# Moving the last stage's norm scaling to GpSimd and its masked factors to ScalarE

## Chip, cores and metric

The kernel runs on one core of a Trainium2 chip. The metric is device time in microseconds for one launch, the median of several runs. The engines are TensorE (PE in the profile; PEld is its weight load), VectorE (DVE), ScalarE (ACT), GpSimd (POOL) and SyncE (SP, which here only issues transfers). Each engine works through its own queue in order; engines meet through semaphores.

## What is computed

Four graph layers over x of shape (128, 128, 128): 128 batches of 128 nodes with 128 features, with a 0/1 adjacency of the same shape. Each layer is `x = x + layer(relu(layernorm(x)))`. The change touches only the part of the kernel that computes the end of layer 1 and all of layers 2 and 3. Cut to what matters:

```
# end of layer 1: y is normalised over all batches, leaky relu, second half of the product with Wt, added to x
# layer 2 (four heads) and layer 3 (one head, followed by elu):
h  = max(layernorm(x), 0)
Wh = h @ W (+ b)
e  = leaky_0.2(Wh.a_i[:, None] + Wh.a_j[None, :])
e  = where(adj > 0, e, very negative)
x  = x + softmax(e) @ Wh            # layer 3: x + elu(softmax(e) @ Wh)
```

## The kernel before

The batches are worked in 32 groups of four (`G = 4`), each held as a tile of 128 nodes by four batches by 128 features. Two long stages come first: layer 0 with the pairwise differences of layer 1, until about 1500 us, and the scores and softmax of layer 1, until about 2317 us. The last stage begins there and ends with the kernel; it finishes layer 1 and does layers 2 and 3 for one group after another, with several groups in flight. Its code is `attention(g)`.

`attention(g)` does no work itself. It lists steps: a name, an engine, a cost in microseconds, the steps that must come before, the PSUM banks that it takes and gives back, and the work. `_planned` merges the lists of all groups into a single order: it repeatedly takes the step that could start first by these costs, with an allowance of 0.2 us from engine to engine, a release of one more group every `PERIOD = 12` us (five at the beginning), four single PSUM banks (`ONE = 4`) and two double ones (`TWO = 2`). The work is issued in that order, so the costs decide how each engine's queue is sorted; what the chip then takes is another matter. SBUF tiles rotate through rings (`BUFS`: seven for h, ten for off, five for right2, two for right3).

The steps of a group, with the lines of the profile:

- lz and lx load y and x (SP); for five groups they are on the chip already. off (line 1190, GpSimd) turns the stored uint8 mask M8 into a bf16 tile that is 1 where there is no edge and 0 where there is one. M8 holds only 0 and 1, written as `adj > 0`.
- y (line 1193, ScalarE), yl (line 1195, VectorE), po (line 1201, TensorE) and x1 (line 1204, VectorE) finish layer 1.
- Then `layer(n, ...)` runs for layer 2 and, after the attention of layer 2 and its addition x2, for layer 3. mv (lines 1217 and 1219, VectorE) takes mean and variance. rs (lines 225, 226, 1223 and 1224, GpSimd) makes the inverse root rs and the shift nb = -mean x rs. h (line 1229, ScalarE) is relu(x rs + nb), four instructions of 128x128, as scale and shift differ by batch. pt (line 1235, TensorE) transposes h into PSUM; hT (line 1304, ScalarE) copies it back; pr (lines 1241 and 1244) multiplies by the weights.
- v (line 1252, VectorE) takes the score columns, w1 (lines 1257, 1258 and 1261, GpSimd) prepares the ones beside the values and wr (lines 1267 and 1270, ScalarE) copies the values. sp (lines 1283 and 1285, GpSimd) splits the scores into three bf16 pieces, and pe (line 1290, TensorE) transposes them.
- left (line 1312, ScalarE) copies the first half of pe. right (line 1296, VectorE) spreads the second half over four parts, each multiplied by its column of a 0/1 tile `own`, so that each part keeps only the rows of its own head or batch.
- ps (lines 1332 and 1335 in layer 2, 1372 and 1375 in layer 3, TensorE) adds the scores, left times right, and the mask: off times a diagonal of a very negative number.
- e (lines 1318 and 1319, ScalarE: two exponentials), em (line 1322, VectorE: the larger of the two), w and pv (lines 1345 and 1381, TensorE), o (lines 1359, 1360, 1385 and 1386, VectorE), x2 (line 1365) and in layer 3 ex (line 1395, ScalarE), x3 and x4 (lines 1396 and 1398, VectorE). out stores x (SP).

Line 960, in the stage before, makes another tile from the same mask with a product and a sum on GpSimd.

Of the kernel before, what the change touches and what calls it, by code (L numbers as in the profile page):

```python
# [11 lines left out]
BF16 = mybir.dt.bfloat16  # L12
U8 = mybir.dt.uint8
AF = mybir.ActivationFunctionType
OP = mybir.AluOpType
AX = mybir.AxisListType

P = 128
G = 4
# [149 lines left out]
def tile_gnn_stack(ctx: ExitStack, tc: tile.TileContext, a: dict, out: bass.AP):  # L169
    nc = tc.nc  # L170
# [46 lines left out]
    M8 = [res.tile([P, G, P], U8, tag=f"m{g}", name=f"m{g}") for g in range(NG)]  # L217
# [44 lines left out]
    with tc.tile_pool(name="c0", bufs=1) as c0, tc.tile_pool(name="p0", bufs=2) as p0, ExitStack() as ctx0:  # L262
# [383 lines left out]
        with tc.If(nc.values_load(flag, min_val=0, max_val=1) > 0) as cmp, \  # L646
# [6 lines left out]
            for g in range(NG):  # L653
                x = pr.tile([P, G, P], F32, name="x")
# [5 lines left out]
                hT = pr.tile([P, G, P], F32, name="hT")  # L660
# [111 lines left out]
    with tc.tile_pool(name="bn", bufs=1) as bn:  # L772
# [3 lines left out]
        last = bn.tile([P, 1], F32, name="last")  # L776
# [41 lines left out]
    with tc.tile_pool(name="c1", bufs=1, reuse_waits="tile") as c1, \  # L818
# [8 lines left out]
        own = c1.tile([P, 1], F32, name="own")  # L827
# [19 lines left out]
        for n in range(2):  # L847
            t = c1.tile([P, G, 1 + 2 * KH], F32, name=f"sk{n}")
# [296 lines left out]
    with tc.If(nc.values_load(bounded, min_val=0, max_val=1) > 0) as cmp, \  # L1145
# [10 lines left out]
        def attention(g):  # L1156


            t, steps = {}, []

            def step(name, engine, cost, after, work, takes=(), last=()):
                steps.append(((g, name), engine, cost, [(g, n) for n in after], takes, last, work))

            def sb(name, shape, dtype=F32):
                t[name] = p3.tile(shape, dtype, tag=name, bufs=BUFS[name], name=name)
                return t[name]
# [20 lines left out]
            lx = () if on_chip else ("lx",)  # L1187

            def masked():
                nc.gpsimd.tensor_scalar(sb("off", [P, G, P], BF16), M8[g], 0.0, None, op0=OP.is_equal)  # L1190

            step("off", "Pool", 1.5, lx, masked)
            step("y", "ACT", 0.75, () if on_chip else ("lz",), lambda: nc.scalar.activation(
                t["y"], t["y"], AF.Identity, bias=bias2, scale=scale2[:, 0:1]))
            step("yl", "DVE", 0.65, ("y",), lambda: nc.vector.scalar_tensor_tensor(
# [2 lines left out]
            def rest():  # L1198
                po = bank("po")
                for k in range(G):  # L1200
# [4 lines left out]
                 last=("po",))  # L1205

            def layer(n, heads, wx, first):

                q = lambda name: name + str(n)
                N = P + 2 * heads  # L1210
                mv, rs, nb = q("mv"), q("rs"), q("nb")
# [14 lines left out]
                def normed():  # L1226
                    h = sb("h", [P, G, P])
                    for k in range(G):
                        nc.scalar.activation(h[:, k, :], t["x"][:, k, :], AF.Relu, bias=t[nb][:, k:k + 1],  # L1229
                                             scale=t[rs][:, k:k + 1])  # L1230

                def turned():
                    pt = bank(q("pt"))
# [59 lines left out]
                rows, own = (32 * G, own_h) if first else (32, own_k)  # L1293

                def right():
                    nc.vector.tensor_tensor(sb(q("right"), [P, 4, P], BF16)[0:rows],
                                            t[q("pe")][0:rows, 1:2, :].to_broadcast([rows, 4, P]),
                                            own[0:rows, :, None].to_broadcast([rows, 4, P]), OP.mult)

                step(mv, "DVE", 1.05, ("x1",) if first else ("x2",), moments)  # L1300
                step(rs, "Pool", 1.7, (mv,), root)
                step(q("h"), "ACT", 1.2, (rs,), normed)
                step(q("pt"), "PE", 0.5, (q("h"),), turned, takes=(q("pt"),))
                step(q("hT"), "ACT", 0.52, (q("pt"),), lambda: nc.scalar.copy(sb(q("hT"), [P, G, P]), t[q("pt")]),
                     last=(q("pt"),))
                step(q("pr"), "PE", 1.0, (q("hT"),), projected, takes=("2" + q("pr"),))
                step(q("v"), "DVE", 0.3, (q("pr"),), scores)
# [3 lines left out]
                step(q("pe"), "PE", 0.2, (q("sp"),), crossed, takes=(q("pe"),))  # L1311
                step(q("left"), "ACT", 0.3, (q("pe"),), lambda: nc.scalar.copy(
                    sb(q("left"), [P, P], BF16)[0:rows], t[q("pe")][0:rows, 0, :]))
                step(q("right"), "DVE", 0.6, (q("left"),), right, last=(q("pe"),))

            def exps(ps, e):

# [3 lines left out]
            def higher(ps, e):  # L1321
                nc.vector.scalar_tensor_tensor(t[e], t[e], TINY, t[ps], op0=OP.max, op1=OP.max)  # L1322

            layer(2, 4, w2x, True)
            for k in range(G):
                ps, e, pv = f"ps{k}", f"e{k}", f"pv{k // 2}"
# [39 lines left out]
                t["x"], t["o2"], -1.0, t["x"], op0=OP.add, op1=OP.add))  # L1366

            layer(3, 1, w3x, False)

            def summed3():  # L1370
# [33 lines left out]
        with tc.manual_schedule():  # L1404
            groups = [attention(g) for g in sorted(range(NG), key=lambda g: g not in Y)]
            for work in _planned(groups, PERIOD, {"1": ONE, "2": TWO}):
                work()


    with cmp.Else(), tc.tile_pool(name="c2", bufs=1) as c2, tc.tile_pool(name="p2", bufs=5) as p2, \  # L1410
# [25 lines left out]
        left = c2.tile([3, 4], F32, name="left")  # L1436
# [188 lines left out]
```

## Time and profile before

| what | value |
|---|---|
| median of 3 runs | 2777.38 us (2776.46 to 2777.83) |
| profiled execution | 2781.11 us, of which span 2779.3 us |
| granted TensorE clock, mean | 0.968 |
| PE busy over the span | 2457.4 us (88%) |
| DVE busy | 2472.0 us (89%) |
| ACT busy | 2388.7 us (86%) |
| POOL busy | 1724.0 us (62%) |
| last stage, 2317 to 2777 us: busy PE, DVE, ACT, POOL | 402.2, 381.1, 382.6, 252.7 of 460 us |

The profiled execution is one run, 3.7 us above the median of the others. Busy shares are averages over three stages with different limits, so only the last row speaks of the stage around the change. Where instructions of an engine follow each other closely, their durations overlap, and the distance from start to start says what one of them costs the engine.

### The profile page before, as it was taken

To read this page: it belongs to the slowest core of one execution; us is meant where nothing else is said; L and a number is where in the kernel's file an instruction comes from. 1 tells how busy PE (TensorE), PEld (TensorE's weight loads), DVE (VectorE), ACT (ScalarE), POOL (GpSimd) and SP (SyncE) were. 2 spreads that over 40 slices of the span, in tenths; PEclk is the share of its full clock that TensorE was granted. 3 is DMA by queue.
4 is the path that set the end of the run, shared out by engine and by line. 5 is a ranking of instruction groups with operands and counts; after the bars stand their busy time and mean duration, and the time that the engine had idled before them with its cause. 6 is when DMAs were issued, how large, how long until landed. Compare 5 with 4: busy or idle time off the path is not lost.

```text
span 2779.3 us, 42065 instructions
## 1 busy us (share of the span) xinstructions
PE 2457.4 (88%) x14521; PEld 1182.0 (43%) x14521; DVE 2472.0 (89%) x4712; ACT 2388.7 (86%) x2837; POOL 1724.0 (62%) x1629
## 2 busy tenths in 40 slices
PE   3899999999999999999998789888888897999896
PEld 2333333333333333333332344444444445777675
DVE  4899999999999999999999688888888887899976
ACT  4899999999999999999998778778778766899985
POOL 5799999999999999999997001111000115565642
PEclk7999999999999999999999899999999999999998
DMA  7455555555555555555543899999999971121110
GB/s 283 171 223 201 212 201 210 210 212 201 208 201 208 211 209 207 208 207 215 206 193 125 330 409 411 410 411 410 409 410 410 409 266 54 46 69 58 58 31 25
DMA packets 195933, 635.66 MB, mean 229 GB/s; under 512 B 32755, under 2 KB 100470, under 8 KB 132214
## 3 DMA queue, kind: packets, MB, share of 16 engines
q1 hardware_dynamic: 195264, 632.62, 58.6%
q8 instruction: 120, 1.97, 0.3%
q14 instruction: 111, 0.91, 0.1%
q10 hardware_dynamic: 438, 0.17, 0.0%
HBM read 328.84 MB, written 303.89 MB: 228 GB/s over the span
## 4 chain that ended last, share of the span: by engine, by line
ACT 33%; PE 22%; DVE 19%; issue 11%; DMA 10%; POOL 3%; SPq 1%; ACTq 0%; DVEq 0%; POOLq 0%
ACT d L360 11%; ACT z L336 11%; PE hp L322 6%; PE ps L871 5%; DMA rows<-sk 4%; DVE d L312 3%; DMA u<-rows 3%; DVE z L914 3%; DMA z<-hp 3%; PE hp L325 2%; ACT h L1229 2%; PE pk L878 2%; PE pv L1345 2%; ACT o L462 1%; ACT h L503 1%
## 5 line engine op out<-in xcount | busy, mean ns | idle before, releaser
L312 POOL TENSOR_TENSOR d<-xe 128x2048 f32<-128x2048 f32 x256 | 1074.1, 4202 | 67.1 <-PE hp L322 48.9
L322 PE MATMUL hp<-d,w1T 128*64 128x512 f32 x4096 | 999.4, 603 | 119.8 <-ACT z L336 96.8
L360 ACT ACTIVATE d<-d 128x2048 f32<-128x2048 f32 x384 | 734.6, 1935 | 24.7 <-POOL d L312 18.2
L312 DVE TENSOR_TENSOR d<-xe,xp 128x2048 f32<-128x2048 f32 x256 | 579.5, 2264 | 5.8 <-PE hp L322 3.1
L322 PEld LDWEIGHTS hp<-d,w1T 128*64 128x64 f32 x4096 | 286.2, 137 | 640.4 <-issue 466.6
L336 ACT COPY z<-hp 128x1024 f32<-128x1024 f32 x512 | 516.9, 1028 | 47.1 <-PE hp L325 24.4
L962 POOL TENSOR_TENSOR x<-x,bt 128x512 f32<-128x512 f32 x32 | 46.5, 1455 | 672.1 <-DMA x<-x 629.0
L350 DVE BATCH_NORM_STATS2 st<-z 128x6 f32<-128x512 f32 x512 | 349.3, 682 | 42.4 <-ACT z L336 42.1
L351 DVE BATCH_NORM_STATS2 st<-z 128x6 f32<-128x512 f32 (+1 forms) x512 | 329.3, 643 | 0.0
L914 DVE SCALAR_TENSOR_TENSOR z<-z 128x2048 f32<-128x2048 f32 x128 | 296.6, 2317 | 6.5 <-ACT z L896 6.5
L896 ACT ACTIVATE z<-z,bias,scale 128x2048 f32<-128x2048 f32 x128 | 267.1, 2087 | 9.3 <-DVE bias L809 7.7
L325 PE MATMUL hp<-both_t,xw 128*64 128x512 f32 x1024 | 268.3, 596 | 0.0
L900 ACT ACTIVATE zr<-z,bias,scale 128x2048 f32<-128x2048 f32 x128 | 267.3, 2088 | 0.9 <-DMA z<-hp 0.9
L871 PE MATMUL ps<-z,w2z 128*32 128x512 f32 x1024 | 144.7, 638 | 65.1 <-DVE z L914 64.9
L878 PEld LDWEIGHTS pk<-pick,su 128*128 128x128 f32 x1024 | 127.4, 196 | 136.2 <-DVE su L892 94.0
L878 PE MATMUL pk<-pick,su 128*128 128x16 f32 x1024 | 139.9, 269 | 19.9 <-DVE su L892 19.3
L1345 PE MATMUL pv<-wr,e 128*128 128x128 f32 x1024 | 141.7, 285 | 5.8 <-DVE e L1322 4.0
L871 PE MATMUL ps<-z,w2l 128*32 128x512 f32 x1024 | 142.7, 626 | 0.0
L871 PE MATMUL ps<-zr,w2r 128*32 128x512 f32 x1024 | 141.0, 623 | 0.0
L325 PEld LDWEIGHTS hp<-both_t,xw 128*64 128x64 f32 x1024 | 80.7, 138 | 140.7 <-issue 140.7
L1345 PEld LDWEIGHTS pv<-wr,e 128*128 128x128 f32 x1024 | 129.4, 197 | 13.5 <-DVE e L1322 4.1
L1322 DVE SCALAR_TENSOR_TENSOR e<-e,ps 128x512 f32<-128x512 f32 x160 | 106.8, 677 | 25.9 <-ACT ps L1319 25.1
(243 smaller groups left out, 3823.2 us busy)
## 6 DMA issues: line engine op xcount, KB each, us to landing
hp<-z SPq DMA_DIRECT2D x248, 1024.0 KB, 3.9
z<-hp SPq DMA_DIRECT2D x248, 1024.0 KB, 14.2
x<-x SPq DMA_DIRECT2D x118, 256.0 KB, 5.9
u<-rows SPq DMA_DIRECT2D x32, 384.0 KB, 11.6
x<-in_x_dram SPq DMA_DIRECT2D x32, 256.0 KB, 3.1
adj<-in_adj_dram SPq DMA_DIRECT2D x32, 256.0 KB, 3.5
part<-in_adj_dram SPq DMA_DIRECT2D x16, 512.0 KB, 7.6
out_dram<-x SPq DMA_DIRECT2D x32, 256.0 KB, 2.4
```

The lines of the kernel that those rows point to most:

```text
L312: eng.tensor_tensor(d, ahead, x[:, None, None, :].to_broadcast([P, 2, KC, P]), OP.max if t == BY_MAX else OP.subtract)
L322: nc.tensor.matmul(hp[64 * hh:64 * hh + 64, c:c + 512], w1T2 if by_max else w1T, d[:, hh, c:c + 512], start=True, stop=not by_max, skip_gr ...
L325: nc.tensor.matmul(hp[64 * hh:64 * hh + 64, c:c + 512], XW[i // NT // 2][:, i // NT % 2, :], both_t.rearrange("p h k i -> p h (k i)")[:, h ...
L336: nc.scalar.copy(half_of(b, t), linear.pop(i))
L350: nc.vector.bn_stats(st[:, 2 * t, :], hs[:, 0:512])
L351: nc.vector.bn_stats(st[:, 2 * t + 1, :], hs[:, 512:1024 - P * last])
L360: nc.scalar.activation(diffs[i], diffs[i], AF.Abs)
L871: nc.tensor.matmul(ps[32 * c:32 * c + 32, :], w[:, w0:w0 + 32], v[:, 512 * c:512 * c + 512], start=j0 == 0, stop=w is w2r, skip_group_chec ...
L878: nc.tensor.matmul(pk[:, kk, 0:16], su[:, kk, :], pick.rearrange("p h j -> p (h j)"), start=True, stop=True)
L900: nc.scalar.activation(zr, z1, AF.Relu, bias=bias1, scale=scale1[:, 0:1])
L914: nc.vector.scalar_tensor_tensor(z0, z0, 0.01, z0, op0=OP.mult, op1=OP.max)
L1345: nc.tensor.matmul(t[pv][:, k % 2, hd, :], t[e][:, hd, :], flat[:, at:at + P], start=True, stop=True)
```

## The change

Four edits, all in `attention(g)`:

- off is computed as mask x (-1) + 1 instead of mask == 0, still on GpSimd, and its planned cost goes from 1.5 to 0.65.
- h of both layers becomes x rs + nb without relu, four tensor_scalar instructions on GpSimd instead of four activations on ScalarE; planned cost 1.9 instead of 1.2.
- The relu moves into hT, the copy of the transposed h out of PSUM, which stays on ScalarE at the same planned cost.
- right becomes four activations on ScalarE, each with a column of `own` as its scale, instead of one product on VectorE; planned cost 1.4 instead of 0.6.

```diff
             def masked():
-                nc.gpsimd.tensor_scalar(sb("off", [P, G, P], BF16), M8[g], 0.0, None, op0=OP.is_equal)
-
-            step("off", "Pool", 1.5, lx, masked)
+                nc.gpsimd.tensor_scalar(sb("off", [P, G, P], BF16), M8[g], -1.0, 1.0, op0=OP.mult, op1=OP.add)
+
+            step("off", "Pool", 0.65, lx, masked)
...
                 def normed():
                     h = sb("h", [P, G, P])
                     for k in range(G):
-                        nc.scalar.activation(h[:, k, :], t["x"][:, k, :], AF.Relu, bias=t[nb][:, k:k + 1],
-                                             scale=t[rs][:, k:k + 1])
+                        nc.gpsimd.tensor_scalar(h[:, k, :], t["x"][:, k, :], t[rs][:, k:k + 1], t[nb][:, k:k + 1],
+                                                op0=OP.mult, op1=OP.add)
...
                 def right():
-                    nc.vector.tensor_tensor(sb(q("right"), [P, 4, P], BF16)[0:rows],
-                                            t[q("pe")][0:rows, 1:2, :].to_broadcast([rows, 4, P]),
-                                            own[0:rows, :, None].to_broadcast([rows, 4, P]), OP.mult)
+                    to = sb(q("right"), [P, 4, P], BF16)
+                    for part in range(4):
+                        nc.scalar.activation(to[0:rows, part, :], t[q("pe")][0:rows, 1, :], AF.Identity,
+                                             scale=own[0:rows, part:part + 1])
...
-                step(q("h"), "ACT", 1.2, (rs,), normed)
+                step(q("h"), "Pool", 1.9, (rs,), normed)
                 step(q("pt"), "PE", 0.5, (q("h"),), turned, takes=(q("pt"),))
-                step(q("hT"), "ACT", 0.52, (q("pt"),), lambda: nc.scalar.copy(sb(q("hT"), [P, G, P]), t[q("pt")]),
+                step(q("hT"), "ACT", 0.52, (q("pt"),), lambda: nc.scalar.activation(
+                    sb(q("hT"), [P, G, P]), t[q("pt")], AF.Relu),
                      last=(q("pt"),))
...
-                step(q("right"), "DVE", 0.6, (q("left"),), right, last=(q("pe"),))
+                step(q("right"), "ACT", 1.4, (q("left"),), right, last=(q("pe"),))
```

## The prediction

> **What bounds the kernel now.** I read the page's slices first (part 2: each digit is the busy share of a fortieth of the span, in tenths).
>
> ```profile
> PE   3899999999999999999998789888888897999896
> DVE  4899999999999999999999688888888887899976
> ACT  4899999999999999999998778778778766899985
> POOL 5799999999999999999997001111000115565642
> ```
>
> Only the last seven digits belong to the stage that the change touches: there PE, DVE and ACT are all at 8 to 9, POOL at 5 to 6. No engine stands out, so the stage needs a closer ruler than busy shares. I took it from the one-line views of x4 (the last addition of a group) and the busy time of two stretches, the filling of the stage and the rest.
>
> ```profile
> L1398 DVE SCALAR_TENSOR_TENSOR x<-ex,x x32: 647/684/1089, 2381.4 to 2775.0; 128x512 f32<-128x512 f32 x32
> 2381.40:2775.00 393.60, 346.10 (x2511) 276.05 (x2510) 328.53 (x1028) 328.03 (x769) 201.18 (x579) 0.95 0.17 50
> 2317.00:2381.40 64.40, 56.09 (x402) 44.64 (x402) 51.88 (x191) 54.59 (x128) 51.53 (x134) 0.95 0.05 16
> ```
>
> (Numbers after the length: PE, PEld, DVE, ACT, POOL busy us; then clock, DMA share, GB/s.) The 32 groups end between 2381.4 and 2775.0: 393.6 / 31 = **12.70 us per group**. The filling before is 64.4 us. DMA is at 0.17, so loads and stores bind nothing.
>
> Next, what a group costs each engine, by start-to-start spacing of neighbours in the timeline around 2500 us, because durations overlap there:
>
> ```profile
> 2503.96 0.29 ACT L1312 COPY left<-pe 128x128 bf16<-128x128 bf16 x1
> 2504.12 0.62 ACT L1304 COPY hT<-pt 128x512 f32<-128x512 f32 x1
> 2504.60 1.68 ACT L1229 ACTIVATE h<-x,nb,rs 128x128 f32<-128x128 f32 x4
> 2506.15 0.82 ACT L1193 ACTIVATE y<-y,bias,scale 128x512 f32<-128x512 f32 x1
> ```
>
> The reader is to see that four h activations hold ACT from 2504.60 to 2506.15, 1.55 us (0.39 each), left 0.16, hT 0.48. In the same way e with its second exponential takes 0.99, wr 0.53, ex 0.54, y 0.72. **ACT per group**: y 0.72 + h 3.10 + hT 0.96 + wr 1.06 + left 0.32 + five e 4.95 + ex 0.54 = 11.65. **DVE**: a 128x512 operation spaces at 0.60, so yl, x1, x2, x3, x4, two right and five em are 12 x 0.60 = 7.20; two mv at 1.06; two v at 0.15; two o at 0.56 and one at 0.80: 11.54. **PE** at full clock: eight four-matmul f32 steps (po, two pr, four w, pv) at 0.89, two pt 0.45, the bias rows 0.33, two pe 0.22, two ps 0.76, the third layer's ps 0.55: 10.9, and 11.5 at the clock of 0.95. **POOL**: off 1.50, two rs at 1.92, sp 1.36 and 1.24, the memsets 0.37: 8.3. So three engines lie at 11.5 to 11.65 of 12.70, and about 1.05 us per group goes to engines that wait, in their fixed order, for one another:
>
> ```profile
> DVE e L1322 <- ACT ps L1319: 25.1, 31, 2.9
> ACT h L1229 <- POOL nb L1224: 12.8, 19, 1.9
> ACT h L1229 <- POOL wr L1261: 8.0, 6, 2.2
> PE ps L1372 <- DVE right L1296: 7.7, 6, 2.5
> POOL pieces L1283 <- DVE v L1252: 60.6, 21, 7.3
> POOL rs L225 <- DVE mv L1219: 43.9, 18, 7.9
> ```
>
> (Waits from 2330 us: total us, times, longest.) DVE waits for ACT, ACT for POOL's root at h, PE for DVE's right. POOL waits most, but nobody lacks it for long.
>
> **What the Trainium skill says.** "Perfetto Trace Analysis", section "Identifying the Most-Contended Engine", says that matmul busy time is no good measure of the room left on TensorE. The trace agrees: 346.1 of 393.6 us busy is 88%, the same as spacing gives only after division by the clock. "SBUF — State Buffer", section "Who interferes with whom", says that a VectorE operation with two SBUF inputs contends with a GpSimd operation that reads SBUF, one blocking the other. The trace agrees as far as it goes: the root's L226 has 1036 ns as minimum and median but 1556 as maximum, x4 684 and 1089.
>
> **The change part by part.** The rows that price it:
>
> ```profile
> L1229 ACT ACTIVATE h<-x,nb,rs x256: 477/480/593, 2326.3 to 2759.4; 128x128 f32<-128x128 f32 x128
> L1296 DVE TENSOR_TENSOR right<-pe,own_h x32: 669/682/692, 2335.3 to 2717.1; 128x512 bf16<-128x512 bf16 x32
> L1190 POOL TENSOR_SCALAR off<-m x32: 1482/1506/1943, 2318.3 to 2641.3; 128x512 bf16<-128x512 uint8 x32
> L960 POOL TENSOR_SCALAR cap<-m x32: 617/941/2547, 1524.7 to 2284.1; 128x512 f32<-128x512 uint8 x32
> L407 POOL COPY xe<-xe 128x128 f32<-128x128 f32 x64 | 18.7, 292 | 1.9 <-ACT xe L394 1.9
> ```
>
> (Minimum, median and maximum in ns, but for L407, whose second number after the bar is the mean.)
>
> 1. *Off by product and sum.* L960 is that very operation on the same uint8 mask, with f32 out: 617 ns at best, 941 in the middle, in another stage. Against 1506, POOL gains 0.89 us at most, 0.57 by the median, and nothing if a bf16 output is what costs. I take 0.89: the minimum is free of contention, as off's own flat 1482 to 1506 is. Off hides beside other work, except at the start, where four of them (6.0 us) precede the first root: there 2324.26 instead of some 2324.0 when its mv is written, so 0.3 us.
> 2. *Affine part from ACT to POOL.* ACT loses 8 x 0.39 = 3.1 us per group, and with it the wait at h for the root. POOL gains eight tensor_scalar of 128x128 with two pointer operands; the trace has none. Below: the copy at 292 ns. Above: off's slope, (1506 - 233) / 508 ns per element on a 233 ns base (L225, 128x4), gives 544. Cap's slope, (617 - 233) / 508, gives 327 without pointers. "GPSIMD Engine Reference", section "3.1 Elementwise — side-by-side cycle accounting", puts the best loop at about 1.8 cycles per element (769 ns for 512); cap's 617 is better than that. I take 420 ns, a third of the way up, for the pointers and for blocking: 3.4 us per group. Behind these four in POOL's order stand the next memsets, pieces and roots; PE's pt waits for them instead of for ACT. Path from root to pt: 4 x 0.42 = 1.7 against 1.55 and a hop, nothing either way.
> 3. *Relu in hT's copy.* The same 128x512 read of PSUM; 588 ns now. Nothing, plus or minus 0.07 (L475, an ACTIVATE form, has 661 and 595).
> 4. *Right from DVE to ACT.* DVE loses 2 x 0.60 = 1.2 us per group. ACT gains eight 128-column activations from PSUM. "ScalarE: Activation LUTs", section "What ACT_TABLE_LOAD costs", gives 186 ns + 0.833 ns per column, 93 more per pointer operand, neighbours overlapping by 93; the trace agrees (h: 186 + 107 + 186 = 479, measured 480; left: 293, measured 282). With one pointer that is 386 ns, spaced at 0.29: 1.16 per layer, 2.3 per group. Below: left's spacing of 0.16, 1.3 per group; above: h's 0.39, 3.1, if the zero bias is fetched as a pointer too. Behind right on ACT wait the next e; for right wait ps2 and ps3 on PE and the release of the pe bank. That bank is held 1.16 us after left instead of 0.60 and a hop: some 0.4 more, twice per group, of four banks; small.
> 5. *The order.* The planner sorts each engine's queue by these costs. Its own sums are now ACT 12.26 (was 11.86), POOL 10.85 (was 7.9), DVE 10.76, period 12: ACT slightly over, which lets the oldest ready group go first, as before. SP's loads keep their costs and stay ahead.
>
> **Sum.** ACT 11.65 - 3.10 + 2.32 = 10.9. DVE 11.54 - 1.2 = 10.3. POOL 8.3 - 0.89 + 3.36 = 10.8. PE 11.5 as before. The tightest engine falls from 11.65 to 11.5, the second from 11.54 to 10.9, the third to 10.8. If only the tightest counts, a period shrinks by 0.15; if PE's load is not what sets it, by ACT's 0.75. I take 0.4, since two of the three engines that blocked one another get room while POOL, new among the full ones, gives some back: 31 x 0.4 = 12.4 us. The profiled execution took 2781.1 (span 2779.3 and 1.8 around it), which makes 2768.7; the median of the runs is 3.7 lower, so **2765.0**. The main case runs from 31 x 0.2 to 31 x 0.95 us, 2748 to 2771.
>
> **Rivals.** *POOL becomes the bound (slower).* Mechanism: eight affine operations and two roots in one in-order queue. POOL without h is 7.4; with the 1.05 lost to waits it reaches 12.70 when h costs (11.65 - 7.4) / 8 = 0.53 us each. My upper price is 0.544, blocking by DVE's four two-input additions can add 0.1, and an off that saves nothing shifts the point to 0.42. At 0.58 POOL has 12.05, period 13.1: +12.4 us, 2790; with off unchanged and 0.544, 12.65: +31, 2808. For it: POOL's queue is serial and had 104 us of slack in waits for v and mv, which now delay h as well. Against it: cap's 617. *PE is the bound already:* the three relieved engines only wait longer for it, at most 31 x 0.15 = 4.7 us, 2773; for it stands 11.5 of 12.70, against it that PE waits for DVE and ACT in the list above. *The move to ACT saves nothing:* right at 0.39 puts ACT at 11.65 again, and only DVE is relieved: 2775.
>
> **How the numbers follow.** Main case 0.5; PE or ACT unchanged as the bound 0.2; POOL the bound 0.3 (2783 to 2808). About 0.2%, 5.5 us, is what a measurement of this kernel can tell from no change. Of the 0.2, a quarter passes that line downwards: faster 0.55, same 0.15, slower 0.30. Leaving a tenth on either side gives 2740 to 2802, for the main case alone 2748 to 2771.
>
> **What would show it.** Right: x4's first and last start some 12.3 us apart per group; h on POOL at 0.35 to 0.48 by spacing; off near 0.62; the four right activations within 1.2 us; ACT and DVE idle in more places, most of it behind PE. Wrong: POOL at over nine tenths of the last stage and PE's pt waiting for h at L1229 by tens of us (the slower rival), ACT waiting hardly less than before with right at 0.39 (the last one), or a period unchanged with PE without gaps.

## The result and the profile after

The changed kernel takes 2786.41 us (median of 11 runs, 2781.86 to 2792.14) against 2776.28 us (11 runs): ratio 1.0037, 95% interval 1.0029 to 1.0045. It is slower by 10 us where 12 us of gain were forecast. The profiled execution took 2792.14 us (span 2790.3), the longest of the eleven, so its totals lie some 6 us above the median.

First the slices of the profile's page, of the changed kernel:

```profile
PE   3899999999999999999997888988888887898897
DVE  4899999999999999999998788888888886787776
ACT  4899999999999999999998878878778755887776
POOL 5799999999999999999996001111011117877864
```

In the last seven digits POOL went from mostly 5 and 6 to 7 and 8, DVE and ACT fell by about one. The relief took place. PE, which got no work and lost none, is not denser for it. The one-line view of x4 (now line 1400) and the windows, with the columns as before; the last two lines are the whole stage, of the changed kernel and of the kernel before:

```profile
L1400 DVE SCALAR_TENSOR_TENSOR x<-ex,x x32: 657/688/824, 2372.3 to 2786.1; 128x512 f32<-128x512 f32 x32
2372.30:2786.10 413.80, 364.82 (x2621) 290.30 (x2619) 310.50 (x1014) 320.53 (x814) 302.40 (x829) 0.94 0.16 49
2315.00:2372.30 57.30, 45.70 (x293) 35.81 (x293) 37.65 (x140) 34.04 (x84) 51.44 (x139) 0.88 0.02 8
2315.00:2788.00 473.00, 410.52 (x2912) 326.11 (x2912) 348.83 (x1155) 354.57 (x896) 353.84 (x968) 0.93 0.14 44
2317.00:2777.00 460.00, 402.19 (x2912) 320.69 (x2912) 381.11 (x1219) 382.62 (x896) 252.71 (x712) 0.95 0.15 45
```

The first group ends 57.3 us after the stage's start instead of 64.4, but then 413.8 / 31 = 13.35 us go by per group instead of 12.70. These two stretches don't hold the same work: 293 of PE's 2912 instructions fall into the filling where it was 402. So the whole stage is the better measure, 473 us against 460.

Of these 13 us, 8 are PE's own: the same 2912 instructions keep it busy for 410.5 us instead of 402.2, at a granted clock of 0.93 instead of 0.95. That is one execution of each kernel. The medians are hardly to be explained so: over all whole executions the mean granted clock is 0.970 in the changed kernel, and 0.971 both in e9, which is 23 us faster (see below), and in the kernel before as it ran beside e9. A clock lower by 0.02 in this stage, a sixth of the span, would make 0.003 there.

The rows that priced the parts (minimum, median, maximum in ns; last the group view, whose number before the second bar is the mean):

```profile
L1229 POOL TENSOR_SCALAR h<-x,rs,nb x256: 445/452/1400, 2324.2 to 2769.6; 128x128 f32<-128x128 f32 x128
L1190 POOL TENSOR_SCALAR off<-m x32: 614/620/1052, 2316.2 to 2666.6; 128x512 bf16<-128x512 uint8 x32
L1298 ACT ACTIVATE right<-pe,own_h x128: 342/390/453, 2332.6 to 2749.0; 128x128 bf16<-128x128 bf16 x128
L1305 ACT ACTIVATE hT<-pt x64: 570/597/673, 2326.4 to 2771.5; 128x512 f32<-128x512 f32 x64
L1229 POOL TENSOR_SCALAR h<-x,rs,nb 128x128 f32<-128x128 f32 x256 | 129.5, 519 | 1.8
```

off, right and hT came out as priced. h is 452 ns in the middle but 519 in the mean, 129.5 / 256 = 0.51 us of GpSimd each. The trace says which ones are long. Of the 256, 196 overlap none of VectorE's operations that take both inputs from SBUF (yl, x2, x3 and x4), and last 452 ns in the mean, 457 at most. The 60 that do overlap one last 740 in the mean. The waits from 2330 us on (total us, times, longest) have changed hands; the last line is of the kernel before:

```profile
PE pe L1290 <- POOL pieces L1283: 23.8, 16, 3.1
ACT left L1314 <- PE pe L1290: 21.4, 22, 3.1
ACT hT L1305 <- PE pt L1235: 16.0, 22, 4.0
DVE sums L1361 <- PE pv L1347: 44.1, 32, 4.8
POOL pieces L1283 <- DVE v L1252: 23.8, 10, 5.9
POOL rs L225 <- DVE mv L1219: 19.3, 10, 6.1
PE pe L1290 <- POOL pieces L1283: 3.8, 4, 2.1
```

ACT no longer waits for POOL, but PE does: at pe, for the pieces, 23.8 us against 3.8 before. And as PE's queue is in order, ACT and DVE wait behind it. One such wait, in the timelines of POOL, DVE, PE and ACT around 2410 us (start, length, engine, instruction):

```profile
2407.45 4.53 POOL L1229 TENSOR_SCALAR h<-x,rs,nb 128x128 f32<-128x128 f32 x8
2408.64 0.25 DVE L1252 COPY v<-pr 128x16 f32<-128x16 f32 x2
2411.96 0.21 POOL L1283 CAST pieces<-v 128x32 bf16<-128x32 f32 x1
2413.45 0.28 PE L1290 MATMUL pe<-ident_b,pieces 128*128 128x128 bf16 x2 [1.09 <-POOL pieces L1283]
2413.78 0.27 ACT L1314 COPY left<-pe 128x128 bf16<-128x128 bf16 x1 [1.75 <-PE pe L1290]
```

The scores v are there at 2408.9, yet their pieces begin at 2411.96: two groups' h, eight instructions in 4.53 us, stand ahead of them in GpSimd's queue. PE stands still for 1.09 us, ACT for 1.75.

Two causes can lie behind this picture. Either GpSimd has too much work (**load**), or its work is sorted badly because the planner believes it to be shorter than it is (**costs**). Waits alone don't tell them apart, so the experiments do. In the expectations load is called theory Q, the order theory O and later, as costs, theory C. R puts the loss on right, P on TensorE's own work, D on the planner's period.

### The profile page after: what moved, and what is told of

Its sections match the earlier page's. It is cut to its first block, busy times and chain, and to the rows that moved or that the text cites. A ratio compares the mean times of both kernels' runs of the same rounds, so it can differ in the third digit from the quotient of the medians.

```text
span 2790.3 us, 42280 instructions
## 1 busy us (share of the span) xinstructions
PE 2463.1 (88%) x14521; PEld 1187.5 (43%) x14521; DVE 2440.4 (87%) x4648; ACT 2361.3 (85%) x2837; POOL 1826.4 (65%) x1885
## 4 chain that ended last, share of the span: by engine, by line
ACT 27%; PE 23%; DVE 18%; DMA 12%; issue 11%; POOL 8%; ACTq 0%; DVEq 0%; SPq 0%; POOLq 0%
ACT z L336 10%; ACT d L360 10%; PE hp L322 5%; PE ps L871 5%; DVE d L312 4%; DMA z<-hp 4%; DMA rows<-sk 4%; DMA u<-rows 3%; DVE z L914 2%; POOL h L1229 2%; PE hp L325 2%; PE pv L1347 2%; PE pk L878 2%; DVE st L350 1%; POOL rs L226 1%
## 5 line engine op out<-in xcount | busy, mean ns | idle before, releaser
L1347 PE MATMUL pv<-wr,e 128*128 128x128 f32 x1024 | 148.6, 293 | 6.8 <-DVE e L1324 5.6
L1229 POOL TENSOR_SCALAR h<-x,rs,nb 128x128 f32<-128x128 f32 x256 | 129.5, 519 | 1.8
## 6 DMA issues: line engine op xcount, KB each, us to landing
u<-rows SPq DMA_DIRECT2D x32, 384.0 KB, 11.6
```

Source lines behind the costliest of these rows:

```text
L1347: nc.tensor.matmul(t[pv][:, k % 2, hd, :], t[e][:, hd, :], flat[:, at:at + P], start=True, stop=True)
```

## The experiments

Each was timed beside the kernel before. us are medians; ratios are to the kernel before as it ran beside that version, with 95% intervals.

| run | us | ratio | planned GpSimd us per group |
|---|---|---|---|
| before | 2775.1 to 2777.4 | 1 | 7.9 |
| the change | 2786.4 | 1.0037 (1.0029 to 1.0045) | 10.85 |
| e1_off | 2777.8 | 1.0006 (0.9997 to 1.0014) | 7.05 |
| e2_h | 2796.1 | 1.0072 (1.0058 to 1.0085) | 11.7 |
| e3_right | 2808.9 | 1.0121 (1.0103 to 1.0138) | 7.9 |
| e5_old_order | 2818.3 | 1.0148 (1.0133 to 1.0164) | 7.9 |
| e6_after_short_root | 2759.6 | 0.9945 (0.9930 to 0.9960) | 10.85 |
| e7_before_short_root | 2761.6 | 0.9951 (0.9937 to 0.9964) | 7.9 |
| e8_before_extra | 2847.8 | 1.0253 (1.0238 to 1.0268) | 7.9 |
| e9_true_costs, period 12.6 | 2763.4 | 0.9958 (0.9944 to 0.9972) | 12.6 |
| e10_after_period 12.6 | 2792.2 | 1.0064 (1.0051 to 1.0078) | 10.85 |
| e11_after_costs, period 12 | 2768.0 | 0.9973 (0.9963 to 0.9983) | 12.55 |
| e12_before_period 12.6 | 2772.9 | 0.9991 (0.9982 to 1.0001) | 7.9 |
| e13_before_true, period 12.6 | 2767.1 | 0.9969 (0.9960 to 0.9978) | 9.2 |
| e14_no_nb, period 12.6 | 2815.5 | 1.0139 (1.0122 to 1.0156) | 11.4 |
| e15_true_124, period 12.4 | 2763.4 | 0.9954 (0.9939 to 0.9969) | 12.6 |
| e16_before_costs, period 12 | 2766.5 | 0.9965 (0.9953 to 0.9977) | 9.2 |
| e17_lower_costs, period 12 | 2809.1 | 1.0118 (1.0103 to 1.0134) | 9.05 |
| e18_nb_on_dve, period 12.4 | 2771.7 | 0.9979 (0.9972 to 0.9986) | 11.4 |
| e19_before_nb_on_dve, period 12.4 | 2786.0 | 1.0038 (1.0025 to 1.0052) | 8.0 |

The last column is summed from the costs in the code: off + 2 rs + 2 h (where GpSimd has it) + 2 memsets of 0.3 + 2 sp. The change is 0.65 + 3.4 + 3.8 + 0.6 + 2.4.

### The parts alone

e1_off is the first edit alone, cost included; e2_h the second and third; e3_right the body of right alone, everything in the order of before; e5_old_order has all bodies of the change, but the labels and costs of before:

```diff
# e5_old_order, against the change
-                step(q("h"), "Pool", 1.9, (rs,), normed)
+                step(q("h"), "ACT", 1.2, (rs,), normed)
...
-                step(q("right"), "ACT", 1.4, (q("left"),), right, last=(q("pe"),))
+                step(q("right"), "DVE", 0.6, (q("left"),), right, last=(q("pe"),))
...
-            step("off", "Pool", 0.65, lx, masked)
+            step("off", "Pool", 1.5, lx, masked)
```

> Only off by product and sum, with its planned cost of 0.65. Theory Q (POOL's queue: eight affine operations in one in-order queue make the pieces late for PE's pe): off itself is harmless, 0 to 5 us faster than before. Theory O (the planner's new order is the worse one): any change of costs reshuffles the queues, so this may move by 5 us or more either way. Theory R (right on ScalarE holds PSUM banks and ACT too long): 0 to 5 us faster.

> Only h to GpSimd, with relu in hT and its planned cost of 1.9; off stays is_equal, right stays on VectorE. Theory Q: POOL carries 0.8 us per group more than in the changed kernel, so slower than it: 20 us or more over before, with POOL at over nine tenths and PE waiting for pieces. Theory O: about as slow as the changed kernel, +5 to +15. Theory R: no slower than before, since right is where it was: -10 to +2.

> Only right as four activations on ScalarE, every step in the order of before. ACT then has 11.65 + 2.3 = 13.95 us per group, DVE 10.3. Theory Q and O: ACT becomes the bound, 1.3 us or more per group over 12.70, +35 to +60 us, and this says what right costs when h stays on ACT too. Theory R: beyond that ACT load, PE's ps and pe wait for right by tens of us: over +60 us.

> All edits of the change, but planned with the labels and costs of before, so that the instructions are issued in the order of before. Theory Q: still slower than before, +5 to +25, with PE waiting for POOL's pieces. Theory O: the loss is gone, 5 to 20 us faster than before. Theory R: still slower, with PE or ACT waiting for right and for pe banks rather than for pieces.

off is worth nothing by itself. right alone costs 32 us on an ACT that also has h, a little less than worked out, and PE waits for it in ps3 for 21.4 us up to the end: no ground for theory R, which wanted over 60. h alone loses 20 us, with POOL waiting for just 45 of some 475 us: as theory Q had it. e5 lies outside all that was expected. The same instructions in the old order lose 42 us instead of 10, more than Q allowed, and theory O as it was put down (in the old order the loss is gone) is refuted: that order was made for h on ACT and right on VectorE. POOL waits longer there than in the change (98 us against 68). More idle time on the engine that is said to be full, and a worse result: the order counts by tens of microseconds.

### GpSimd's load, taken off and put on

```diff
# e6 and e7, against the change and against before: the power of the root left out
-                    rsqrt(sb(rs, [P, G]), t[mv][:, :, 1])
+                    nc.gpsimd.tensor_scalar(sb(rs, [P, G]), t[mv][:, :, 1], 0.0, 0.3, op0=OP.mult, op1=OP.add)
...
# e8, against before: four more instructions in root, after nb
+                    spare = sb("spare", [P, G, P])
+                    for k in range(G):
+                        nc.gpsimd.tensor_scalar(spare[:, k, :], t["x"][:, k, :], t[rs][:, k:k + 1], t[nb][:, k:k + 1],
+                                                op0=OP.mult, op1=OP.add)
```

> The changed kernel with the power left out of the root in both layers of the last stage: rs is a constant 0.3, written by the one tensor_scalar, so every norm there is scaled wrongly and POOL is spared two L226 of 1.04 us with their gaps, 2.2 us per group; order and all else stay. In the changed kernel POOL stands still for 68 of 473 us, so it is occupied for (473 - 68) / 32 = 12.65 us per group. Theory Q (POOL's whole occupation is the bound): POOL falls to 10.4, the next engine sets the pace, and the kernel is 20 to 40 us faster than the changed one, thus 10 to 30 faster than before. Theory P (the room on ACT and DVE is worth nothing, TensorE's own work sets the pace and h is late on its path): gain of the shorter path only, 0 to 10 us against the changed kernel, not faster than before.

> The control: the kernel before with the same power left out (rs a constant 0.3, the norms of the last stage wrongly scaled). Theory Q: POOL is not the bound there, occupied for (460 - 158) / 32 = 9.4 us per group, so 0 to 8 us faster, the waits of h for the root. Theory P: the same. If it gains 20 us or more, the root's length on the path counts by itself, and the run before says nothing on POOL's load.

> The kernel before with the four affine instructions of h added on GpSimd behind each root, into a spare tile that nobody reads; h stays on ScalarE. Nothing is moved, POOL alone gets 8 x 0.51 = 4.05 us per group more: 9.4 + 4.05 = 13.4 of a period that was 12.70. Theory Q: slower by 15 to 40 us. Theory P: 0 to 8 us slower, as no step on TensorE's path is longer.

e6 and e7 leave out a part of the computation and are there for the comparison alone. e6 gains 27 us on the change and 16 on before, which looks like Q. The control takes half of that away: before gains 14 us from the same edit, more than the 8 expected of an engine with 158 us to spare. With a short root the two kernels are equal, 0.9945 and 0.9951. Nor does e6 tell load from costs: with the root shortened GpSimd is occupied for 10.0 us per group, and the plan's 10.85 is no longer too short. e8 loses 72 us, some three times what its load explains: 13.4 us of work per group where 12.70 went by should cost 32 x 0.7 = 22. What load does not explain, the plan may: it still counts 1.7 us for a root that now takes 3.7. That was not tested.

### The plan's costs

In the changed kernel's trace rs takes 2.15 us, a split 1.49 and four h 2.02 in the mean, from the start of the first instruction to the end of the last; the plan says 1.7, 1.2 and 1.9. Only numbers in the plan differ in these runs:

```diff
# e9 (period 12.6) and e15 (period 12.4), against the change
-PERIOD, FIRST, HOP, LANDING = 12, 5, 0.2, 3.0
+PERIOD, FIRST, HOP, LANDING = 12.6, 5, 0.2, 3.0
...
-            step("off", "Pool", 0.65, lx, masked)
+            step("off", "Pool", 0.7, lx, masked)
...
-                step(rs, "Pool", 1.7, (mv,), root)
-                step(q("h"), "Pool", 1.9, (rs,), normed)
+                step(rs, "Pool", 2.05, (mv,), root)
+                step(q("h"), "Pool", 2.1, (rs,), normed)
...
-                step(q("sp"), "Pool", 1.2, (q("v"),), split)
+                step(q("sp"), "Pool", 1.5, (q("v"),), split)
...
-                step(q("right"), "ACT", 1.4, (q("left"),), right, last=(q("pe"),))
+                step(q("right"), "ACT", 1.2, (q("left"),), right, last=(q("pe"),))
# e10: PERIOD alone.  e11: rs, h and sp alone.  e17: rs 1.35, h 1.55, sp 1.0 alone
# against before: e12 PERIOD alone.  e13: rs 2.05, sp 1.5, PERIOD.  e16: rs 2.05, sp 1.5 alone
```

> The changed kernel planned with what its trace shows: off 0.7, rs 2.05, h 2.1, sp 1.5, right 1.2, a period of 12.6. Only the order differs. Theory Q: within 8 us of the changed kernel, still slower than before. Theory O (the planner sorted badly because its GpSimd costs were too low): 10 us or more faster than the changed kernel.

> The changed kernel with nothing but the planner's period at 12.6 instead of 12; its costs stay as they are in the change. Theory C (GpSimd steps planned too short put the pieces behind the affine parts): the loss stays, within 6 us of the changed kernel. Theory D (groups released every 12 us on engines that need more than 12 pile up): most of the gain of the run with true costs comes back, 2760 to 2770.

> The changed kernel with nothing but GpSimd's costs as its trace shows them (rs 2.05, h 2.1, sp 1.5) at the old period of 12. Theory C: the gain of the run with true costs comes back, 2758 to 2770. Theory D: within 6 us of the changed kernel.

> Control: the kernel before with the period at 12.6. Theory C: within 6 us of before. Theory D: within 6 us too if before has no pile, 8 to 15 faster if the period helps any kernel of this kind; then the run with true costs owes its gain to that and not to the change.

> Control: the kernel before with rs 2.05 and sp 1.5 in the plan and the period at 12.6. If replanning alone is worth as much as the run with true costs showed (12 us), the change is worth nothing at its best; both C and D expect less than 6 us, since POOL stands idle for 158 of 460 us there.

> The changed kernel with all true costs (off 0.7, rs 2.05, h 2.1, sp 1.5, right 1.2) at a period of 12.4: a third order made from true costs. Costs as the cause: 2758 to 2770, as the other two. Luck of one order: anywhere from 2755 to 2795.

> The kernel before with rs 2.05 and sp 1.5 in the plan, period 12 as it was. If costs are what counts there too: 2765 to 2770. If its gain needs the period as well: within 5 us of before.

> The changed kernel with GpSimd's steps planned still shorter: rs 1.35, h 1.55, sp 1.0, period 12. Costs as the cause: a larger loss than the change's, 2790 to 2820. Luck of one order: anywhere, also faster than the change.

With costs that fit, the change is faster than before by 12 us; the period alone does nothing for it (2792), the three GpSimd costs alone do (2768). It goes by dose, and for three different plans with fitting costs: planned at 9.05 us per group 2809, at 10.85 2786 and 2792, at 12.55 and 12.6 2768, 2763 and 2763. e5 fits at the low end, planned at 7.9, though h and right are planned on the wrong engines there too. So it is the costs and not the luck of one order. No run plans GpSimd above 12.6, so whether costs must fit or need only be high enough is open. The profile of e9, its x4, its window of steady work, h and the wait at pe (in the same views as above); the last two lines are of e10:

```profile
L1400 DVE SCALAR_TENSOR_TENSOR x<-ex,x x32: 650/690/779, 2375.1 to 2756.7; 128x512 f32<-128x512 f32 x32
2375.10:2756.70 381.60, 345.37 (x2534) 272.97 (x2532) 298.88 (x974) 309.08 (x791) 302.95 (x819) 0.96 0.17 52
L1229 POOL TENSOR_SCALAR h<-x,rs,nb 128x128 f32<-128x128 f32 x256 | 129.7, 519 | 0.2
PE pe L1290 <- POOL pieces L1283: 8.1, 7, 2.7
PE pe L1290 <- POOL pieces L1283: 7.3, 7, 2.2
PE pt L1235 <- POOL h L1229: 7.3, 8, 1.6
```

381.6 / 31 = 12.31 us per group. h costs GpSimd as much as before the replanning (129.7 against 129.5 us), and its other work is the same too; over the stage POOL waits for 37 us of 445 where it waited for 68 of 473. The load is unchanged and the engine fuller, and yet the kernel is 23 us faster. So the load alone did not make the loss; the order did.

By which path the order did it is shown in part only. In e9 PE waits for pieces for 8.1 us instead of 23.8, and all of PE's waits for GpSimd together fall from 28.5 to 11.6 us. But in e10, which is as slow as the change, PE waits for pieces for 7.3 us, and for GpSimd in all for 15.8. The queue tells the same: between the arrival of the scores and their first piece GpSimd works off 126 h instructions in the change, summed over all 64 splits, 86 in e9, and 86 in e10 too. The late pieces belong to the loss of the change, and are not all that a plan with short costs does.

The controls matter as much. Before gains 9 us too from true costs of rs and sp, with the period (0.9969) or without (0.9965), where less than 6 was expected, and 3 us that can't be told from nothing from the period alone. Planned alike, change and before are at 0.9954 to 0.9973 and at 0.9965 to 0.9969. That the change as such gains anything is not shown.

### What is left of GpSimd's load

```diff
# e14, against the true plan at 12.6 (root planned at 1.45, four buffers for mv2 and mv3): the two nb instructions left out
-                        nc.gpsimd.tensor_scalar(h[:, k, :], t["x"][:, k, :], t[rs][:, k:k + 1], t[nb][:, k:k + 1],
-                                                op0=OP.mult, op1=OP.add)
+                        nc.gpsimd.tensor_scalar(h[:, k, :], t["x"][:, k, :], t[mv][:, k, 0:1], t[rs][:, k:k + 1],
+                                                op0=OP.subtract, op1=OP.mult)
# e18, against the true plan at 12.4, and e19, against before with true costs at 12.4: nb as a step of its own,
# its two instructions in root left out, root planned at 1.45, four buffers for mv, rs and nb
+                def shifted():
+                    nc.vector.scalar_tensor_tensor(sb(nb, [P, G]), t[mv][:, :, 0], -1.0, t[rs], op0=OP.mult, op1=OP.mult)
...
+                step(nb, "DVE", 0.2, (rs,), shifted)
```

> The changed kernel with true GpSimd costs, period 12.6, and h as (x - mean) x rs, so that the two instructions for nb fall away on GpSimd (root planned at 1.45; four buffers for mv2 and mv3). POOL loses 2 x 0.58 = 1.2 us per group of some 12.3. If POOL's load is what is left: 8 to 25 us faster than with true costs alone (2763), so 2738 to 2755. If TensorE and the order set the pace now: within 6 us of it.

> The changed kernel with true costs at a period of 12.4, and nb = (mean x -1) x rs as one VectorE instruction between root and h (planned 0.2), so that GpSimd loses two small instructions per layer, 1.2 us per group, and h keeps the product-and-sum form at 0.45; four buffers for the small norm tiles. If POOL's load is what is left: 2740 to 2756, against 2763 with the same plan and nb on GpSimd. If not: 2758 to 2768.

> The control: the kernel before with rs 1.45 and sp 1.5 planned, a period of 12.4 and nb on VectorE in the same way. POOL has room there, so only the wait of ACT for the root can change: 2760 to 2770, as with true costs alone (2767).

e14 failed for a reason of its own, in its one-line view of h:

```profile
L1227 POOL TENSOR_SCALAR h<-x,mv,rs x256: 787/798/2141, 2322.2 to 2795.3; 128x128 f32<-128x128 f32 x128
```

In this form h takes 798 ns instead of 452. GpSimd got 8 x 0.35 = 2.8 us more per group for the 1.2 that it lost, and the plan did not know. The run says nothing on a lighter GpSimd. In e18 GpSimd did become lighter: POOL's idle time rose to 99 us, where e15, with the same period and nb on GpSimd, has 47. The time did not fall (2771.7 against 2763.4), and lies outside both ranges expected. That does not clear GpSimd's load. The control e19 lost 19 us by the same edit (2786 against 2767), though GpSimd had room there, so the move has a price of its own: PE's waits for VectorE, 34 us in e13, are 48 in e19. In e18 that price may hide what the lighter queue gains. Whether GpSimd's load is part of what is left stays open. Shifts of 5 to 20 us from one plan to another are the size of anything still to be gained here. The fastest versions that compute everything are e9 and e15, some 12 us faster than before and 23 than the change.

## Why the prediction was wrong, point by point

- **What bounds (TensorE at 11.5, no engine alone):** mis-sized. In the stage before, TensorE is busy for 402.2 us, 12.6 per group, VectorE for 11.9 and ScalarE for 12.0 (381.1 and 382.6 / 32). So TensorE was the fullest, and not the third behind ScalarE's 11.65. The spacing of 0.89 for a step of four matmuls was a floor (around 2510 us others take up to 1.04), and the ruler of 12.70 us per group was too short: between the first and the last x4 lie 2511 of 2912 TensorE instructions, the work of 27.6 groups and not of 31. (Nor is the 88% that TensorE was busy there the same as the spacings give after division by the clock: 11.5 of 12.70 is 91%.) By the same token e9's 12.31, close to the forecast 12.3, proves little.
- **Off (0.89 less):** right, 620 ns for 1506, and worth nothing by itself (e1).
- **Right on ACT (2.3 per group):** right. Four take 1.09 to 1.21 us from the first's start to the last's end around 2510 us, 390 ns one by one in layer 2 and 343 in layer 3.
- **hT:** right, 599 for 588 in the mean.
- **h on GpSimd (0.42 each):** too low. (The 420 ns lie half-way between the bounds named, 292 and 544, and not a third of the way up.) Alone it is 452, and beside VectorE's operations with two inputs from SBUF some take up to 1400: 0.51 in all, 4.05 us per group and not 3.36. The contention that the Trainium skill describes ("SBUF — State Buffer", section "Who interferes with whom": a VectorE instruction with two SBUF inputs contends with a GpSimd instruction that reads SBUF) was priced inside the 0.42 and was larger. This trace agrees with the page: all 36 h instructions over 480 ns overlap such an operation.
- **GpSimd before (8.3):** too low as well. It stood still for 158 of 460 us, so it was occupied for (460 - 158) / 32 = 9.4: the spacings of single steps, picked where nothing disturbed them, missed 1.1. (Of this 0.3 is the end of the kernel, 10 us after GpSimd's last instruction.) The sum for after should have been 9.4 - 0.8 + 4.05 = 12.65, which is what (473 - 68) / 32 gives, and not 10.8.
- **The order (nothing):** the first step that failed. The prediction set the planner's sums beside each other, found ACT slightly over its period, and let it pass that POOL's plan said 10.85, since its own sum for POOL, 10.8, was short by the same amount. It never held the plan's costs for rs and sp against the trace it had just read (1.92 and 1.3 against 1.7 and 1.2). POOL's plan was 1.8 us per group short of the chip. Put right, that is worth 18 to 23 us (e11, e9, e15) to the change. Before gets 9 by the same means, so 9 to 14 of the 22 us between forecast and result go to the order.
- **The relief (0.4 us per group, 12.4 in all):** the second. Planned alike, the change lies between 1 us behind before (2768.0, e11, against 2766.5, e16) and 4 ahead (2763.4, e9, against 2767.1, e13). That fits TensorE's 12.6: the work went from the two engines that were less full to one that then had 12.65. But no run takes work off TensorE, and e18 does not settle GpSimd's share, so why the relief is worth so little is argued and not shown.
- **The rivals:** the slower one named the right engine and queue, and its crossing point lay too high, since it started from 7.4 instead of 8.6. Its own sign, PE's pt waiting for h by tens of us, did not come (2.3 us, its weight loads 11.0); PE waited for pieces. And it blamed the load, while e9 carries the same load and is faster than before. That the relief of ACT and DVE buys little is what the rival with TensorE as bound said: at most 4.7 us.
- That e9 and e15 land at 2763, close to the 2765 forecast, does not save the sum: 9 of their 12 us before gets from the same replanning.

## What to carry to other kernels

When a list scheduler with costs of its own sets the order, a moved step is two changes, its work and the plan, and the plan's costs have to be checked against the trace before the load is summed. Occupation is best read over a whole stage, as span less waits or as busy time, per group; the spacing of undisturbed neighbours gave a floor here, for GpSimd and for TensorE, and the stretch from the first to the last output held less than all the work. And a gain that comes from replanning has to be offered to the kernel before as well, or it is put down to the wrong edit.

## What the hardware showed that was not expected

- On GpSimd, tensor_scalar on 128x128 f32 takes 452 ns in the median as product and sum with two contiguous columns (445 at least), and 798 ns as difference and product with a column of the interleaved mean and variance tile (787 at least). Whether the operations or the stride of the operand make it was not separated.
- off with a bf16 output takes 614 ns at best, as the same operation with f32 output does (617): is_equal without a second operation took 1506, so the bf16 output is not what made it slow.
- GpSimd's 128x128 tensor_scalar takes 452 ns in the mean beside all of VectorE's work but that with two inputs from SBUF (196 instructions, 457 at most), and 740 beside that (60 instructions).
- An idle engine was no sign of room here: POOL waited for 98 us in e5 and 68 in the change, 37 in the faster e9.
